# Loading the adjacency matrix in pieces of two tiles

## Chip, core and metric

The kernel runs on one core of a Trainium2 chip. The metric is the device time of one execution in microseconds; the kernel before took 733.56 us, the median of three runs (727.32 to 735.38).

The core has a tensor engine (TensorE, in the profile PE; its weight loads are PEld), a vector engine (VectorE, DVE), a scalar engine (ScalarE, ACT), GpSimd (POOL), and 16 DMA engines that queues on SP, ACT and POOL feed.

## The reference

Two graph layers over 3327 nodes with 512 features. `adj` is a sparse 3327 x 3327 matrix held densely in fp32, more populated towards low node numbers. Cut to what matters:

```python
# layer 0
h = max(layernorm(x), 0)
x = x + (adj @ (relu(adj @ (h @ W1) + b1) @ W2) + b2)
# layer 1
h = max(layernorm(x), 0)
attn_a = sigmoid(concat(adj @ h, h) @ Wa.T + ba)      # attn_b the same, with Wb and bb
hs = h @ W_sa
e = where(adj != 0, exp(-leaky_relu(s_left[:, None] + s_right[None, :])), 0)
x_a = (e / (sum(e, axis=1) + 1e-5)) @ hs
x_b = adj @ (h @ W_gcnb) + b_gcnb
x = x + sigmoid(attn_a * x_a + attn_b * x_b)
```

`adj` is thus used as a dense matrix in two successive products of layer 0, and layer 1 needs the places of its nonzero entries.

## The kernel before

The nodes are padded to 3328, which is 26 blocks of 128, and `adj` comes in transposed as `adjT`. The output columns of a pass are cut into chunks of 512 (`CW`); 3328 is six and a half of them, so one chunk has a width of 256.

**First pass** (lines 549 to 600). For each chunk, from the last columns to the first, TensorE sums `acc_u` over the 26 row blocks `j`: `u[j]`, which is `h @ W1` of block `j`, against the tile of `adjT` at rows `j` and the chunk's columns (line 568). The same tiles serve the lists of nonzeros: VectorE takes for each row and each group of 32 columns the largest absolute value (line 572), into `most[:, group, j]`. In the first chunk the loads of x, the layer norm, the transposes and the products that make `u` are woven in between.

When a chunk ends, `make_g` takes its sum with relu on ScalarE (line 343), transposes it and copies it to `g`; `make_lists` is made for the chunk and advanced, one step behind each tile, through the next chunk: flags from `most`, a running count (line 452), two small matmuls (lines 465 to 476), masks `at` on VectorE (line 502), short matmuls with these masks into `p_list` (line 513), and `past`, `jb`, `row_h` and `row_a` on VectorE (lines 519 to 532), the numbers of the rows that are to be gathered. GpSimd issues gathers of parts of `adjT` by these numbers (line 166), each paced behind a matmul of the pass. The generator's statements stand in the program where the loop calls it, but the tile framework's scheduler orders the instructions of each engine anew from its own estimate of times, with the constraints that `queued` and `issue_after` set.

**Second pass** (lines 818 to 856). For the dense chunks (four of width 512 and one of 256) TensorE sums `acc_g` over the blocks in the order of the chunks of the first pass, `g[j]` against the tile of `adjT` (line 825). The two other chunks are summed from gathered rows (`acc_s`, line 784). Between these matmuls stand `px` (line 663), which makes x of layer 1 from a finished chunk, its layer norm, and `acc_hub` (line 709), the first block's sums of layer 1. x is loaded again on SP's queue (line 648), and the rows of h are stored there (line 637).

**Layer 1** follows, with the gathered rows only: `acc` (line 981), transposes, `p_b` (line 1035), `p_a` (line 1042) and the output. It doesn't use the dense tiles.

Both passes load the tiles through `load_adj` (line 271), one DMA on SP's queue for each call, 256 KB: one tile in a full chunk and two in the half-width one. Its pool `adjp` has eight buffers of 128 x 512 fp32. A load waits until every instruction that used its buffer is done: the matmul, and in the first pass the maximum too. SP's queue is in order, so what stands behind a waiting load waits with it.

Of the kernel before, what the change touches and what calls it, by code (L numbers as in the profile page):

```python
# [9 lines left out]
F32 = mybir.dt.float32  # L10
AF = mybir.ActivationFunctionType
ALU = mybir.AluOpType
# [4 lines left out]
AX = mybir.AxisListType  # L17

P = 128
CW = 512  # L20
GW = 32
# [29 lines left out]
def kernel(  # L51
# [17 lines left out]
    nc = tc.nc  # L69
    NP, D = x.shape  # L70
    HID = W1.shape[1]
    NB = NP // P
# [25 lines left out]
    def bank(pool, name):  # L98
        return pool.tile([P, CW], F32, tag="bank", name=name)
# [116 lines left out]
    def gather_behind(matmul):  # L216

        g = next(columns, None)
        if g is not None:
            pace(g, matmul)  # L220

    def queued(*insts):

        behind = ExitStack()
        for inst in insts:
            if inst is not None:
                behind.enter_context(tc.issue_after(inst.ins))
        return behind
# [30 lines left out]
    with (  # L259
        tc.tile_pool(name="l0", bufs=1) as l0,  # L260
        tc.tile_pool(name="l0w", bufs=2) as l0w,
        tc.tile_pool(name="adjp", bufs=8) as adjp,
    ):

        def load_adj(j, c, name, n=1):

            c0, w = c
            t = adjp.tile([P, CW], F32, tag="adj", name=f"{name}_{c0}_{j}")
            t = t[:, : n * w].rearrange("p (k i) -> p k i", i=w)
            rows = adjT[j * P : (j + n) * P, c0 : c0 + w]  # L270
            nc.sync.dma_start(t, rows.rearrange("(k p) i -> p k i", p=P))
            return t
# [22 lines left out]
        def load_weights():  # L295
            nc.scalar.dma_start(W2_sb, W2)
            nc.scalar.dma_start(b2_row, b2.partition_broadcast(P))
            nc.scalar.dma_start(W_sa_sb, W_sa.rearrange("(k p) f -> p k f", p=P))
            nc.scalar.dma_start(w_own, w_self.partition_broadcast(P))
            nc.scalar.dma_start(bab_row, b_ab.partition_broadcast(P))  # L300
# [4 lines left out]
        x_loaded, scaled, h_turned, u_made = {}, {}, {}, {}  # L305

        def load_x(i):
            xs[i] = l0w.tile([P, D], F32, tag="x", name=f"x_{i}", bufs=5)
            x_loaded[i] = nc.sync.dma_start(xs[i], x[i * P : (i + 1) * P, :])

        def normalize(i):

            hs[i] = l0w.tile([P, D], F32, tag="h", name=f"h_{i}", bufs=GR // NU)
            with tc.high_priority():
                scaled[i], _ = ln_relu(
                    hs[i], xs.pop(i), l0w, f"a{i}", [scaled.get(i - 2)],
                    [h_turned.get(i - 3), u_made.get(i - 4)],
                    [h_turned.get(i - 2), u_made.get(i - 3)],
                )

        def turn_h(i):
            h = hs.pop(i)
            pt = bank(psB, f"pt_{i}")
            for k in range(KD):
                nc.tensor.transpose(pt[:, k * P : (k + 1) * P], h[:, k * P : (k + 1) * P], ident)  # L325
            hs[i] = hTs[i % 2]
            h_turned[i] = nc.scalar.copy(hs[i].rearrange("p k n -> p (k n)"), pt)

        def make_u(i):
            hT = hs.pop(i)  # L330
            pu = bank(psB, f"pu_{i}")
            for k in range(KD):
                nc.tensor.matmul(  # L333
                    pu[:, :HID], hT[:, k, :], W1_sb[:, k, :], start=(k == 0), stop=(k == KD - 1)
                )
            u_made[i] = nc.scalar.copy(u[i], pu[:, :HID])
# [212 lines left out]
        for n, c in enumerate(back):  # L549
            c0, w = c  # L550
            acc = bank(psA, f"acc_u_{c0}")
            per = CW // w
            most = l0w.tile([P, MG, NB], F32, tag="most", name=f"most_{c0}")
            for j in range(NB):
                if n == 0:
                    if j + 4 < NB:
                        load_x(j + 4)
                    if j + 3 < NB:
                        normalize(j + 3)
                    if j + 2 < NB:  # L560
                        turn_h(j + 2)
                    if j + 1 < NB:
                        make_u(j + 1)
                if j % per == 0:
                    with queued(x_loaded[min(j + 4, NB - 1)] if n == 0 else None):
                        tile_a = load_adj(j, c, "a1", per)
                a = tile_a[:, j % per, :]
                added = nc.tensor.matmul(  # L568
                    acc[:, :w], u[j], a[:, :w], start=(j == 0), stop=(j == NB - 1)
                )  # L570
                with queued(scaled[min(j + 3, NB - 1)] if n == 0 else None):
                    nc.vector.tensor_reduce(  # L572
                        most[:, : w // GW, j], a[:, :w].rearrange("p (b i) -> p b i", i=GW),
                        axis=AX.X, op=ALU.max, apply_absolute_value=True,
                    )
                if j >= 2:
                    next(lists, None)
                if j % 4 if w == CW else j % 2:
                    gather_behind(added)
                if n == 0 and j % 2 == 0:  # L580
                    with queued(scaled[min(j + 3, NB - 1)]):
                        next(constants, None)
            for work in (lists, constants):
                for _ in work:
                    pass
            chunk_end = make_g(c, acc)
            with tc.issue_after(chunk_end.ins):
                if n == 1:
                    load_weights()
                if 0 < n <= HUB_LOADS:  # L590
                    load_hub(n - 1)
                for i in OWN:
                    if n and c0 <= i * P < c0 + w:
                        load_own(i)
            lists = make_lists(n, most)
            next(lists)
# [208 lines left out]
        def next_late():  # L805
            while late:
                try:
                    next(late[0])
                    return
                except StopIteration:  # L810
                    late.pop(0)
# [6 lines left out]
        for c, (c0, w) in enumerate(dense_chunks):  # L818
            last = c == len(dense_chunks) - 1
            acc = bank(psA, f"acc_g_{c0}")  # L820
            per = CW // w
            for n, j in enumerate(order):
                if n % per == 0:
                    a = load_adj(j, (c0, w), "a2", per)
                added = nc.tensor.matmul(  # L825
                    acc[:, :w], g[j], a[:, n % per, :], start=(n == 0), stop=(n == NB - 1)
                )
                if c == 0 and n >= 2:
                    next(lists, None)
                if n in SUMS.get(c, ()):  # L830
                    next(summing)
                elif c and n % 4:
                    gather_behind(added)
                if n % 2 or (c in (2, 3) and n % 4 == 2):
                    with queued(last_e[0] if last and n < 8 else None):
                        next_late()
                if last and n >= NB - QUIET:
                    continue
                if c > 1 and n % 3 == 2:
                    next(hubs)  # L840
                elif c > 1 and (n > 8 if last else n % 3 == 1):
                    with queued(last_row[0] if last else None):
                        make_e_hub()
            if c == 0:
                for _ in lists:
                    pass
                nc.vector.tensor_reduce(overflow, size, axis=AX.X, op=ALU.max)
            if last:
                with queued(last_e[0]):
                    nc.scalar.activation(root, eps, AF.Sqrt)  # L850
                while late:
                    next_late()
            sT = l0w.tile([HID, CW], F32, tag="gT", name=f"sT_{c0}", bufs=3)
            nc.scalar.copy(sT[:, :w], acc[:, :w])
            late.append(make_h1((c0, w), sT, last))
# [47 lines left out]
    with tc.tile_pool(name="spw", bufs=2) as spw:  # L903
# [175 lines left out]
        with queued(made[1]):  # L1079
            ty, _ = copy_out(0, acc_hub)  # L1080
# [7 lines left out]
        for i in range(NB - 2, 1, -1):  # L1088
# [8 lines left out]
            b, ty, es = turning  # L1097
# [19 lines left out]
        b, ty, es = turning  # L1117
# [19 lines left out]
        ty, _ = copy_out(1, taken[1]["acc"], True)  # L1137
# [3 lines left out]
    with tc.If(over > 0):  # L1141
        with (
# [19 lines left out]
            for c0, w in listed_chunks:  # L1162
                acc = bank(psA, f"acc_again_{c0}")
                for j in range(NB):
                    a = load_some(j, c0, w, "a5")
# [5 lines left out]
                for b in range(w // P):  # L1171
                    i = c0 // P + b
# [23 lines left out]
        with (  # L1196
# [25 lines left out]
            for c in range(len(chunks)):  # L1222
                c0, w = chunks[c]
# [10 lines left out]
                for j in range(NB):  # L1234
                    a = load_all(j, c, "a3")
# [9 lines left out]
                for j in range(NB):  # L1245
                    a = load_all(j, c, "a4")
# [10 lines left out]
                for b in range(w // P):  # L1257
                    i = c0 // P + b
# [63 lines left out]
```

## Time and profile before

The profiled execution took 834.5 us, of which 832.8 us are its span. It is one execution under the profiler; the median of the timed runs is 733.56 us.

| | before |
|---|---|
| median of three runs | 733.56 us |
| profiled execution, its span | 834.5 us, 832.8 us |
| matmuls busy (PE) | 735.6 us, 88% |
| VectorE busy | 506.0 us, 61% |
| ScalarE busy | 194.5 us, 23% |
| GpSimd busy | 461.1 us, 55% |
| loads of adj tiles | 286, 256 KB each |
| maxima (line 572) | 182, of them 156 over 512 elements |
| matmuls of the first pass (line 568) | 161.0 us |
| matmuls of the second pass (line 825) | 117.1 us |
| bytes read from HBM, and mean rate of all DMA | 162.29 MB, 222 GB/s |

A row of the groups reads: line, engine, operation, output and input with their shapes, how often; then busy time and mean ns of one; then the idle time of the engine just before them and what ended most of it. An fp32 matmul leaves two records. A row of the chain that ended last gives start, length and what was on the path. A row of waits gives who waited for whom, the total, how often, and the longest. Busy time counts whatever an engine does, on the path or beside it, so the profile is best read stage by stage.

### The profile page before, as it was taken

The numbers are of one execution on the slowest core, as the hardware profiler recorded it, in microseconds if no ns is written. First come the engines' busy times: TensorE is split into PE (matmuls) and PEld (weight loads), VectorE is DVE, ScalarE is ACT, GpSimd is POOL, SyncE is SP. The second block draws the span as 40 slices with busy tenths as digits, with TensorE's granted clock in tenths as the row PEclk, the third lists the DMA queues.
The fourth block names the chain that finished last, engine by engine and source line by source line (L and its number), as shares of the span: only waits on it lengthen the run. The fifth ranks groups of instructions, "written<-read, shape, count | busy, mean of one in ns | idle before, by whom it ended". The sixth has DMA issues, their size and how long they took to land.

```text
span 832.8 us, 11907 instructions
## 1 busy us (share of the span) xinstructions
PE 735.6 (88%) x3595; PEld 404.5 (49%) x3595; DVE 506.0 (61%) x1625; ACT 194.5 (23%) x402; POOL 461.1 (55%) x490
## 2 busy tenths in 40 slices
PE   9999888989899771999899749967999999999995
PEld 7774333444543220444355236633656655665554
DVE  7778868898860611798987225523665557553552
ACT  7770000000000110354544002211212222221121
POOL 2201756766657776534456766674657666767500
PEclk9999989999999875999999969996999999999999
DMA  8788988988878844789994755664667877767510
GB/s 271 245 287 259 326 246 242 293 272 246 232 232 284 262 132 134 240 279 312 327 314 135 241 150 145 199 185 115 195 211 244 255 206 233 240 205 234 178 51 29
DMA packets 104889, 185.08 MB, mean 222 GB/s; under 512 B 18401, under 2 KB 35441, under 8 KB 104818
## 3 DMA queue, kind: packets, MB, share of 16 engines
q1 hardware_dynamic: 66544, 113.43, 41.8%
q0 software_dynamic: 23264, 57.64, 24.3%
q10 hardware_dynamic: 15010, 13.18, 4.9%
q8 instruction: 30, 0.49, 0.2%
q14 instruction: 41, 0.34, 0.1%
HBM read 162.29 MB, written 22.26 MB: 222 GB/s over the span
## 4 chain that ended last, share of the span: by engine, by line
PE 72%; DVE 7%; issue 6%; another core or an unknown queue 6%; DMA 5%; ACT 2%; POOL 1%; SPq 1%; DVEq 0%; ACTq 0%; POOLq 0%
PE acc_u L568 17%; PE acc L981 12%; PE p_b L1035 11%; PE p_a L1042 10%; PE acc_g L825 8%; PE pu L333 3%; PE ptt L995 3%; DMA a<-in_adjT_dram 2%; PE acc_hub L709 2%; PE px L663 2%; PE pt L325 1%; DMA xb<-in_x_dram 1%; PE acc_s L784 1%; DMA hr<-h_rows,row_h 1%
## 5 line engine op out<-in xcount | busy, mean ns | idle before, releaser
L166 POOL DMA_INDIRECT ae<-in_adjT_dram,row_a x194 | 202.6, 1044 | 181.8 <-DVE past L519 54.3
L568 PE MATMUL acc_u<-a,rows 128*128 128x512 f32 (+1 forms) x364 | 161.0, 583 | 0.5 <-DMA a<-in_adjT_dram 0.5
L166 POOL DMA_INDIRECT hr<-h_rows,row_h x120 | 122.7, 1022 | 62.5 <-issue 27.4
L825 PE MATMUL acc_g<-a,g 128*128 128x512 f32 (+1 forms) x260 | 117.1, 584 | 7.2 <-DMA a<-in_adjT_dram 6.8
L572 DVE TENSOR_REDUCE most<-a 128x16 f32<-128x512 f32 (+1 forms) x182 | 112.3, 638 | 11.6 <-issue 6.3
L1035 PE MATMUL p_b<-W_g_sb,tyT 128*128 128x257 f32 x416 | 99.3, 391 | 15.8 <-DVE tyT L1010 15.3
L1035 PEld LDWEIGHTS p_b<-W_g_sb,tyT 128*128 128x128 f32 x416 | 77.8, 192 | 46.5 <-DVE tyT L1010 15.6
L166 POOL DMA_INDIRECT rows<-h_rows,row_h x74 | 75.1, 1015 | 44.3 <-PE acc L981 20.9
L568 PEld LDWEIGHTS acc_u<-a,rows 128*128 128x128 f32 x364 | 67.2, 195 | 58.8 <-issue 56.0
L1042 PE MATMUL p_a<-W_sa_sb,tyT 128*128 128x512 f32 (+2 forms) x216 | 94.2, 577 | 0.2
L1010 DVE COPY tyT<-ptt 128x512 f32<-128x512 f32 x51 | 34.8, 685 | 87.0 <-PE p_a L1042 31.7
L825 PEld LDWEIGHTS acc_g<-a,g 128*128 128x128 f32 x260 | 50.0, 200 | 58.5 <-issue 44.9
L981 PE MATMUL acc<-hr,ae 64*64 64x512 f32 x480 | 68.3, 614 | 4.4 <-issue 4.0
L166 POOL DMA_INDIRECT g_row<-g_rows,row_h x48 | 49.0, 1021 | 20.9 <-issue 13.4
L1042 PEld LDWEIGHTS p_a<-W_sa_sb,tyT 128*128 128x128 f32 x216 | 40.7, 189 | 38.8 <-issue 36.9
L884 ACT ACTIVATE f<-f 128x2 f32<-128x2 f32 x26 | 5.3, 203 | 192.4 <-DVE f L883 97.2
L981 PEld LDWEIGHTS acc<-hr,ae 64*64 64x64 f32 x480 | 27.6, 136 | 33.6 <-issue 33.0
L343 ACT ACTIVATE gT<-acc_u,b_col 128x512 f32<-128x512 f32 (+1 forms) x7 | 4.6, 656 | 163.8 <-DMA a<-in_adjT_dram 90.9
L663 PE MATMUL px<-W_sb,sT 128*128 128x512 f32 x52 | 26.7, 650 | 15.4 <-ACT sT L799 12.0
L666 DVE TENSOR_TENSOR xb<-px,xb 128x512 f32<-128x512 f32 x26 | 17.3, 682 | 36.6 <-PE px L663 28.5
L981 PE MATMUL acc<-rows,ae 64*64 64x512 f32 x296 | 37.1, 593 | 2.5 <-issue 2.3
L623 DVE SCALAR_TENSOR_TENSOR junk<-rows,w_rows 128x512 bf16<-128x512 f32 x52 | 35.6, 684 | 3.2 <-ACT rows L244 1.1
(159 smaller groups left out, 945.2 us busy)
## 6 DMA issues: line engine op xcount, KB each, us to landing
a<-in_adjT_dram SPq DMA_DIRECT2D x286, 256.0 KB
h_rows<-rows SPq DMA_DIRECT2D x26, 260.0 KB
x<-in_x_dram SPq DMA_DIRECT2D x26, 256.0 KB
xb<-in_x_dram SPq DMA_DIRECT2D x26, 256.0 KB
x<-xb ACTq DMA_DIRECT2D x26, 256.0 KB
x1b<-x SPq DMA_DIRECT2D x26, 256.0 KB
out_dram<-va SPq DMA_DIRECT2D x25, 256.0 KB
ae<-in_adjT_dram,row_a POOLq DMA_INDIRECT x194
```

What stands on the lines that cost most here:

```text
L166: return nc.gpsimd.indirect_dma_start(out=dst, out_offset=None, in_=table, in_offset=bass.IndirectOffsetOnAxis(ap=rows, axis=0), bounds_ch ...
L333: nc.tensor.matmul(pu[:, :HID], hT[:, k, :], W1_sb[:, k, :], start=(k == 0), stop=(k == KD - 1))
L568: added = nc.tensor.matmul(acc[:, :w], u[j], a[:, :w], start=(j == 0), stop=(j == NB - 1))
L572: nc.vector.tensor_reduce(most[:, : w // GW, j], a[:, :w].rearrange("p (b i) -> p b i", i=GW), axis=AX.X, op=ALU.max, apply_absolute_value ...
L623: return nc.vector.scalar_tensor_tensor(junk, h, 1.0, w_rows[:, s, :], op0=ALU.mult, op1=ALU.mult, accum_out=into)
L663: last_row[2] = nc.tensor.matmul(px, sT[:, b * P : (b + 1) * P], W2_sb, start=True, stop=True)
L825: added = nc.tensor.matmul(acc[:, :w], g[j], a[:, n % per, :], start=(n == 0), stop=(n == NB - 1))
L981: added = nc.tensor.matmul(taken[i]["acc"][h][q * HALF : (q + 1) * HALF, :], both[half_p, q * n + k, :], taken[i][k0][k][half_p, q, :D], s ...
L995: moved = nc.tensor.transpose(pt[:, k * P : (k + 1) * P], ty[h][:, k * P : (k + 1) * P], ident)
L1010: last = nc.vector.tensor_copy(dst, src)
L1035: nc.tensor.matmul(p_b[n][:, :WH], tyT[:, k, 0, :], W_g_sb[:, k, n * WH : (n + 1) * WH], start=(k == 0), stop=(k == KD - 1),)
L1042: last = nc.tensor.matmul(p_a[:, c0:c1], tyT[:, k, 1, :], W_sa_sb[:, k, c0:c1], start=(k == 0), stop=(k == KD - 1),)
```

## The change

Each load of adj takes two tiles in a full chunk and four in the half-width one (512 KB), the last one of a half-width chunk only the two that are left. The pool has four buffers of twice the size, the same bytes as before. From the second chunk of the first pass on, one instruction of VectorE takes the maxima of two tiles; in the first chunk it is one tile for each instruction as before. The matmuls are the same.

```diff
-        tc.tile_pool(name="adjp", bufs=8) as adjp,
+        tc.tile_pool(name="adjp", bufs=4) as adjp,
...
-            t = adjp.tile([P, CW], F32, tag="adj", name=f"{name}_{c0}_{j}")
+            t = adjp.tile([P, 2 * CW], F32, tag="adj", name=f"{name}_{c0}_{j}")
...
-            per = CW // w
+            per = 2 * CW // w
...
                 if j % per == 0:
                     with queued(x_loaded[min(j + 4, NB - 1)] if n == 0 else None):
-                        tile_a = load_adj(j, c, "a1", per)
+                        tile_a = load_adj(j, c, "a1", min(per, NB - j))
...
-                with queued(scaled[min(j + 3, NB - 1)] if n == 0 else None):
-                    nc.vector.tensor_reduce(
-                        most[:, : w // GW, j], a[:, :w].rearrange("p (b i) -> p b i", i=GW),
-                        axis=AX.X, op=ALU.max, apply_absolute_value=True,
-                    )
+                both = 2 if n else 1
+                if j % both == 0:
+                    tiles = tile_a[:, j % per : j % per + both, :]
+                    with queued(scaled[min(j + 3, NB - 1)] if n == 0 else None):
+                        nc.vector.tensor_reduce(
+                            most[:, : w // GW, j : j + both],
+                            tiles.rearrange("p k (b i) -> p b k i", i=GW),
+                            axis=AX.X, op=ALU.max, apply_absolute_value=True,
+                        )
...
-            per = CW // w
+            per = 2 * CW // w
             for n, j in enumerate(order):
                 if n % per == 0:
-                    a = load_adj(j, (c0, w), "a2", per)
+                    a = load_adj(j, (c0, w), "a2", min(per, NB - n))
```

## The prediction

> **What bounds the kernel now.** I read the page first for the totals and then cut the span at the ScalarE evictions of line 343, which end the chunks of the first pass (65.1, 89.6, 124.4, 154.9, 182.5, 212.5 and 231.6 us). The windows view of these stretches, with the busy time of PE, PEld, DVE, ACT and POOL, the granted clock, the DMA share and GB/s, says most:
>
> ```profile
> PE 735.6 (88%) x3595; PEld 404.5 (49%) x3595; DVE 506.0 (61%) x1625; ACT 194.5 (23%) x402; POOL 461.1 (55%) x490
> ```
>
> ```profile
> 65.00:89.50 24.50, 24.50 (x109) 11.09 (x108) 22.15 (x56) 0.69 (x1) 7.09 (x7) 1.00 0.89 280
> 89.50:124.40 34.90, 27.58 (x109) 12.49 (x108) 26.32 (x68) 0.69 (x1) 23.00 (x23) 0.85 0.90 284
> 124.40:154.90 30.50, 26.90 (x109) 11.97 (x108) 25.28 (x65) 0.70 (x2) 19.86 (x21) 0.94 0.86 258
> 154.90:182.50 27.60, 25.72 (x116) 11.81 (x115) 25.01 (x67) 0.67 (x1) 18.70 (x19) 1.00 0.89 277
> 182.50:212.50 30.00, 28.01 (x125) 12.80 (x124) 26.32 (x66) 0.70 (x2) 20.24 (x21) 0.94 0.87 262
> 212.50:231.60 19.10, 16.35 (x152) 12.07 (x151) 15.58 (x52) 0.68 (x2) 12.05 (x13) 1.00 0.71 200
> ```
>
> The second chunk (65.0 to 89.5) has TensorE busy all through: 24.5 us is what its 26 tiles and its share of the lists cost it. The later full chunks take 27.6 to 34.9 us. In them VectorE works 25.0 to 26.3 us, and the DMA engines 0.86 to 0.90 of the time, which is 24.6 to 26.2 us in the three chunks after the one that also brings the weights. So three servers need about 25 us each for a chunk, and what lies above that is their waiting for one another.
>
> The chain that ended last (start, length, what) shows which side gives way where:
>
> ```profile
> 79.02 8.79 PE acc_u L568 x20
> 89.55 4.72 DMA a<-in_adjT_dram
> ...
> 113.91 11.36 PE acc_u L568 x26
> ...
> 135.00 3.58 DMA a<-in_adjT_dram
> ...
> 247.33 4.41 DMA a<-in_adjT_dram
> ...
> 274.24 2.41 DMA a<-in_adjT_dram
> ```
>
> The stretch of 26 records is 13 tiles (two records for each fp32 matmul): 11.36 / 13 = 0.874 us per tile, or 262,144 B / 0.874 us = 300 GB/s that adj alone has to come at. Where the chain leaves TensorE it goes through a load of `a`, whose 256 KB took 2.4 to 4.7 us from issue to landing. The DMA queue's own waits say what those loads wait for (total us, times, longest):
>
> ```profile
> SPq L271 <- PE acc_u L568: 52.9, 58, 3.7
> SPq L271 <- PE acc_g L825: 38.3, 42, 6.4
> SPq L271 <- DVE most L572: 8.3, 6, 2.5
> ```
>
> They wait for buffers, which the matmuls, and sometimes the maxima, give back. The eight buffers are therefore in use, and how early one comes back is the lead that a load has. The maxima by shape:
>
> ```profile
> L572 DVE TENSOR_REDUCE most<-a 128x16 f32<-128x512 f32 x156 | 102.7, 676 | 11.3 <-issue 6.0 <-DMA a<-in_adjT_dram 5.0
> L572 DVE TENSOR_REDUCE most<-a 128x8 f32<-128x256 f32 x26 | 9.6, 408 | 0.3 <-issue 0.3
> ```
>
> **What the Trainium skill says.** "Perfetto Trace Analysis", section "Optimizing Scalar/DVE Operations": an instruction of VectorE on SBUF pays some 60 ns beside its elements, and about twice that in the profiled duration, since part of it overlaps the next. The trace agrees: the chain has two maxima back to back in 1.19 us (0.595 each) and six of the half-width ones in 1.96 us (0.327), so an element costs (0.595 - 0.327) / 256 = 1.05 ns and an instruction 0.059 us. The durations, 676 and 408 ns, give 140 ns. The same page, "DMA Optimizations", names both sides of the load: larger DMAs use the HBM better, smaller pieces let work start sooner. Here the runs stay 2 KB (1 KB in half-width chunks), so I count nothing on the first side. "DMA: Bandwidth & Descriptors", section "Anatomy of one DMA — SWDGE (gpsimd) path", puts most of a 2 us fixed cost in the confirmation of the last byte. It speaks of the other issue path, but the shortest landing here (2.41 us, with 0.87 us for the bytes at 300 GB/s) leaves 1.5 us, which fits.
>
> **The maxima in pairs.** Five chunks of 13 pairs and a half-width one of 13: 78 instructions fewer. At 0.059 us each that is 4.6 us; by the durations, 78 x 0.140 = 10.9 us. I take 4.6 us, since VectorE is nearly always followed at once here, and keep both ends. It lies on the path only where VectorE is the last of the three, and then counts in full (0.8 us a chunk). The pair also has to wait for two tiles, but that moves nothing else: in the order of the built programs the first 36 list matmuls (line 513) need the masks `at` (line 502) that stood behind the maxima of 9 tiles and now stand behind 5 pairs: 9 x 0.595 = 5.36 us against 5 x (1024 x 1.05 ns + 0.059) = 5.67 us, 0.3 us later; the other 12 stood behind 13 maxima (7.74 us) and stand behind 7 pairs (7.94). TensorE has by then passed those tiles. Cost 0 to 0.3 us per chunk, 1 us in all; I take 0.
>
> **The loads in pairs.** 286 issues become 144. SP saves 142 x 0.33 us of issue time (the median on its queue), but SP is no step of the path, so 0. What changes is the lead. Before, a buffer returns when its tile is used and its new tile is needed seven tiles later: 7 x 0.874 = 6.1 us, against 0.33 us to issue plus 2.4 to 4.7 us to land, a slack of 1.1 to 3.4 us. After, a buffer returns when the second of its tiles is used, and is needed six tiles later: 5.2 us; and its landing has 0.87 us more bytes in it: 0.33 + 3.3 to 5.6 us. The slack is -0.7 to +1.6 us. A slack of -0.7 us costs 0.7 us in each round of eight tiles. Behind the first chunk there are 6 chunks in the first pass and 5 in the second, two of them of half width: 10 full chunks x 26 / 8 = 32 rounds. None of them short costs 0, all of them 23 us. The two long landings (4.4 and 4.7) among the four in the chain would be short after the change and the two short ones not, but the chain shows the loaded moments, and the second pass has slower tiles from its second chunk on. I take 14 rounds, under half: 14 x 0.7 = 10 us.
>
> Where a load is late anyway, TensorE now waits for the second tile of a pair before it can start the first, one tile of 0.87 us; the chain has four such places: 3 us (0 to 3.5).
>
> **What moves on SP's queue.** Behind a load that waits for its buffer stand the loads of x and the stores of h rows (lines 648 and 637). In the orders, some of these come one tile earlier and some one tile later against the loads; each is some 0.9 us and they cancel: 0, bounded by 2 us to either side, because two loads of x are on the chain (5.3 us at 376.8, 5.2 at 394.3). The scheduler also puts the last products `junk_w` (line 606) into the first pass, where TensorE waited 0.9 us for one at the start of the second: -0.9 us at best, 0 taken. First chunk: its tile cost is 2.19 us on TensorE (0.44 + 0.89 + 0.86 in the chain), which hides a coarser load.
>
> **Sum.** -4.6 x 0.9 (VectorE is among the last in most, not all, chunks) = -4; +10; +3: +9 us, rounded down to +8. The profiled execution took 834.5 us (span 832.8), 101 us over the median of 733.56. Much of its waiting is absent from timed runs, but the three equal floors are not, so I carry the difference and not the ratio: 733.6 + 8 = **742 us**.
>
> **Rivals.**
> - *VectorE decides.* Its 25.0 to 26.3 us stand above the 24.5 us that TensorE needs in each chunk from the third on; whatever it is relieved of shortens the chunk as long as it remains above TensorE and DMA. That ends not slower: -4.6 to -10.9, middle -8, 726 us. It decides if loads keep landing within 5.2 us less issue, that is if the pair lands in under 4.9 us. For it: TensorE waits at the list matmuls for `at` and `most`. Against: the DMA engines' 24.6 to 26.2 us stand right below, and the saving that is sure is 0.8 us a chunk.
> - *Both are hidden.* Most loads land in the short time (2.4 to 3.6 us, slack 0.4 to 1.6 after), so the lead suffices; VectorE's gain of 4 meets 3 us for the pairs waited for, and 1 us of the order: 733 us. For it: TensorE waited directly for `a` only 0.5 us in the first pass and 6.8 in the second.
> - *Every round is short*: 23 + 3 - 4 = +22, 756 us. It needs landings above 4.9 us throughout, for which only the half of the samples speaks.
> - That the pairs aren't made is excluded: the orders show 13 double-width maxima per chunk and 144 loads.
>
> **Numbers.** Slower by the lead (742): 0.43; all rounds short (756): 0.05; both hidden (733): 0.38; VectorE decides (726): 0.14. Range 726 to 756, both outer cases at its ends. One per cent (7.3 us) is about what a measurement of this kernel tells from no change; the faster case lies just beyond it and half of the slower case's neighbours within it, so: faster 0.12, within 0.42, slower 0.46.
>
> **What would show it.** Right: SP's waits for `acc_u` and `acc_g` grow per load, new waits of TensorE or VectorE for `a` in the first pass of together 5 us or more, chunks longer than before. Wrong: chunks nearer 24.5 us with VectorE at 24 us or less, and a pair that lands under 4.9 us. The maxima should show about 1.2 us for 1024 elements; well above that would take the gain away, well below it would add to it.

## The result

The changed kernel takes 741.38 us (median of 12 runs, 736.99 to 746.98), the kernel before in the same comparison 732.38 us (12 runs): a ratio of 1.0116 with a 95% interval of 1.0083 to 1.0149, so 8.5 us slower by the ratio. A second comparison gave 741.11 against 733.84 us, 1.0106 (1.0062 to 1.0150).

The kernel before takes 732 to 735 us on some chips and 835 us on another, where the granted clock of TensorE is lower (0.95 of full speed against 0.99, means over its runs); the profile shown ahead of the prediction (834.5 us, clock 0.94) looks like the slower kind, and its chain of work has stretches of up to 16.5 us put down to an unknown queue. So the comparisons below are made within runs on one chip, and the profile of the kernel before was taken once more on a faster chip; that execution took 730.81 us, its span 729.1.

The windows view of the first pass behind its first chunk, cut at the ScalarE evictions of line 343 as before (busy time of PE, PEld, DVE, ACT and POOL, clock, DMA share, GB/s), first for the kernel before on a faster chip:

```profile
65.19:89.67 24.48, 24.48 (x108) 11.07 (x107) 22.24 (x56) 0.69 (x1) 7.15 (x7) 1.00 0.90 280
89.67:120.40 30.73, 26.82 (x108) 10.42 (x107) 24.42 (x62) 0.69 (x2) 23.73 (x24) 1.00 0.97 312
120.40:146.82 26.42, 24.87 (x108) 11.05 (x107) 26.42 (x71) 0.68 (x1) 18.70 (x20) 1.00 0.98 304
146.82:172.06 25.24, 25.15 (x116) 11.44 (x115) 25.24 (x67) 0.69 (x2) 19.49 (x19) 1.00 0.98 310
172.06:197.95 25.89, 25.07 (x125) 11.29 (x124) 25.61 (x65) 0.69 (x2) 20.37 (x19) 1.00 0.99 302
197.95:214.99 17.04, 16.09 (x152) 11.92 (x151) 16.49 (x57) 0.68 (x1) 13.08 (x14) 1.00 0.84 239
```

and for the changed kernel (span 739.9):

```profile
65.28:90.17 24.89, 24.71 (x107) 10.60 (x105) 21.18 (x44) 0.69 (x1) 7.15 (x7) 1.00 0.86 270
90.17:124.04 33.87, 29.73 (x108) 12.98 (x109) 26.42 (x56) 0.69 (x1) 23.11 (x23) 0.85 0.93 292
124.04:151.15 27.11, 25.75 (x107) 10.54 (x105) 25.23 (x55) 0.69 (x1) 19.80 (x21) 1.00 0.94 287
151.15:178.95 27.80, 26.13 (x116) 11.41 (x117) 25.72 (x55) 0.69 (x2) 19.26 (x19) 1.00 0.92 281
178.95:206.08 27.13, 25.64 (x125) 11.18 (x124) 24.99 (x53) 0.69 (x1) 19.84 (x20) 1.00 0.94 285
206.08:224.65 18.57, 17.14 (x151) 11.59 (x149) 17.24 (x47) 0.69 (x2) 13.71 (x14) 1.00 0.76 211
```

These six chunks take 149.8 us before and 159.4 after. The second pass, up to its last eviction (line 854, then 858), takes 169.5 us before (384.5 - 215.0) and 170.1 after (394.7 - 224.6; 172.1 in the second profile of the changed kernel). Layer 1 is the same length within 1.3 us. So by these profiles nearly all of the loss lies in the first pass.

In the three full chunks from 120 us on, the kernel before has VectorE busy all the time but 0.3 us, TensorE for 25 of 25 to 26 us, and the DMA engines at 0.98 to 0.99. After the change none of the three is full: VectorE, busy for 25.3 us a chunk in place of 25.8, idles for about 2 us of it, and the DMA share is 0.92 to 0.94. The rate falls from 302 to 310 down to 281 to 287 GB/s. Share and rate fall with any chunk that moves the same bytes in a longer time: the share times the length is 25 to 26 us in all six rows. So they show that time is lost, and not by what.

The chunk from 90 us on, which also brings weights, is 3.1 us longer, and its clock is 0.85 in place of 1.00. Whether its waits led to the lower clock, or the clock to a part of its length, isn't shown. The other five chunks are 6.4 us longer. Over the timed runs the clock of the changed kernel is not lower (0.992 on average against 0.990), so a lower clock doesn't explain its loss.

The chain that ended last, of the changed kernel:

```profile
92.82 9.41 DMA a<-in_adjT_dram
...
124.04 6.63 DMA a<-in_adjT_dram
130.75 4.78 DMA a<-in_adjT_dram
135.55 1.22 DVE most L575
...
145.93 5.59 DMA a<-in_adjT_dram
151.55 1.22 DVE most L575
...
225.62 4.43 DMA a<-in_adjT_dram
```

and two of the loads on the chain of the kernel before, in its new profile:

```profile
191.87 3.49 DMA a<-in_adjT_dram
...
248.76 6.68 DMA a<-in_adjT_dram
```

A landing on the chain now takes 4.4 to 9.4 us, and the maximum of a pair often stands behind it. In the kernel before these landings are 3.5 to 6.7 us. A chain that ended last picks the late loads, so these aren't typical ones. The waits of SP's queue, of the changed kernel:

```profile
SPq L271 <- PE acc_u L568: 73.3, 62, 3.9
SPq L271 <- PE acc_g L829: 72.0, 42, 4.0
SPq L271 <- DVE most L575: 44.9, 42, 4.1
```

For each of 144 loads that is (73.3 + 72.0 + 44.9) / 144 = 1.3 us of waiting for a buffer. The kernel before, on a faster chip too:

```profile
SPq L271 <- PE acc_u L568: 53.6, 101, 1.8
SPq L271 <- PE acc_g L825: 51.8, 71, 3.3
SPq L271 <- DMA a<-in_adjT_dram: 26.2, 26, 2.8
SPq L271 <- DVE most L572: 13.6, 21, 1.6
```

Here it is (53.6 + 51.8 + 13.6) / 286 = 0.4 us. A load is twice as large after the change, so for each tile it is 0.7 against 0.4 us. (The waits put down to another load's landing, 26.2 us here and 12.0 us after the change, are left out of both.) The wait for a buffer is put down to VectorE twice as often as before, 42 times in place of 21. The maxima of the changed kernel, by shape:

```profile
L575 DVE TENSOR_REDUCE most<-a 128x32 f32<-128x1024 f32 x65 | 78.9, 1214 | 17.2 <-DMA a<-in_adjT_dram 16.9
```

### The profile page after: what moved, and what is told of

It reads as the page before. It is cut to its first block, busy times and chain, and to the rows that moved or that the text cites. A ratio compares the mean times of both kernels' runs of the same rounds, so it can differ in the third digit from the quotient of the medians.

```text
span 739.9 us, 11529 instructions
## 1 busy us (share of the span) xinstructions
PE 707.0 (96%) x3595; PEld 392.0 (53%) x3595; DVE 502.2 (68%) x1547; ACT 193.6 (26%) x402; POOL 467.9 (63%) x490
## 4 chain that ended last, share of the span: by engine, by line
PE 73%; DMA 13%; DVE 10%; ACT 2%; issue 1%; POOL 0%; DVEq 0%; SPq 0%; ACTq 0%; POOLq 0%
PE acc_u L568 13%; PE acc L985 13%; PE p_b L1039 13%; PE p_a L1046 12%; DMA a<-in_adjT_dram 8%; PE acc_g L829 7%; PE pu L333 3%; PE ptt L999 3%; DVE most L575 2%; DMA xb<-in_x_dram 2%; PE px L667 2%; DVE junk L627 2%; PE pt L325 2%; PE acc_hub L713 1%; DMA x<-xb 1%
## 5 line engine op out<-in xcount | busy, mean ns | idle before, releaser
L568 PE MATMUL acc_u<-a,rows 128*128 128x512 f32 (+1 forms) x364 | 164.7, 584 | 4.6 <-DMA a<-in_adjT_dram 4.3
L575 DVE TENSOR_REDUCE most<-a 128x32 f32<-128x1024 f32 (+1 forms) x104 | 104.6, 1010 | 17.2 <-DMA a<-in_adjT_dram 16.9
L829 PE MATMUL acc_g<-a,g 128*128 128x512 f32 (+1 forms) x260 | 110.5, 556 | 3.0 <-DMA a<-in_adjT_dram 2.9
L568 PEld LDWEIGHTS acc_u<-a,rows 128*128 128x128 f32 x364 | 64.9, 194 | 62.6 <-issue 43.0
L1039 PE MATMUL p_b<-W_g_sb,tyT 128*128 128x257 f32 x416 | 97.1, 385 | 0.8 <-ACT tyT L1012 0.5
L829 PEld LDWEIGHTS acc_g<-a,g 128*128 128x128 f32 x260 | 47.3, 190 | 52.2 <-issue 40.6
L166 POOL DMA_INDIRECT g_row<-g_rows,row_h x48 | 51.7, 1077 | 20.8 <-issue 12.8
L985 PE MATMUL acc<-hr,ae 64*64 64x512 f32 x480 | 57.1, 593 | 0.0
L343 ACT ACTIVATE gT<-acc_u,b_col 128x512 f32<-128x512 f32 (+1 forms) x7 | 4.6, 657 | 156.7 <-DMA a<-in_adjT_dram 113.2
L985 PEld LDWEIGHTS acc<-hr,ae 64*64 64x64 f32 x480 | 25.9, 134 | 20.1 <-issue 20.0
L999 PEld LDWEIGHTS ptt<-ident,ty 128*128 128x128 f32 x208 | 24.2, 141 | 14.2 <-issue 13.4
```

The lines of the kernel that those rows point to most:

```text
L166: return nc.gpsimd.indirect_dma_start(out=dst, out_offset=None, in_=table, in_offset=bass.IndirectOffsetOnAxis(ap=rows, axis=0), bounds_ch ...
L568: added = nc.tensor.matmul(acc[:, :w], u[j], a[:, :w], start=(j == 0), stop=(j == NB - 1))
L575: nc.vector.tensor_reduce(most[:, : w // GW, j : j + both], tiles.rearrange("p k (b i) -> p b k i", i=GW), axis=AX.X, op=ALU.max, apply_ab ...
L829: added = nc.tensor.matmul(acc[:, :w], g[j], a[:, n % per, :], start=(n == 0), stop=(n == NB - 1))
L985: added = nc.tensor.matmul(taken[i]["acc"][h][q * HALF : (q + 1) * HALF, :], both[half_p, q * n + k, :], taken[i][k0][k][half_p, q, :D], s ...
L999: moved = nc.tensor.transpose(pt[:, k * P : (k + 1) * P], ty[h][:, k * P : (k + 1) * P], ident)
```

## The experiments

The ratios below are to the kernel before on the same chip.

### One part alone: loads in pairs, maxima of one tile

```diff
-                both = 2 if n else 1
+                both = 1
```

> The changed kernel with the maxima of one tile each; only the loads are in pairs. Lead theory: the changed kernel plus the 4 us that the maxima save: 745. Rival, VectorE is hidden: 741. Rival, the maxima of two tiles are what costs: 732.

On the chip with before at 835 us: 839.95 against 835.17 us, 1.0054 (1.0015 to 1.0092).

> Loads in pairs, maxima of one tile. Lead theory as recorded: 745 where before is at 732. If the cost is in the maxima of two tiles and the loads in pairs are hidden: 732 to 736. If each part alone makes the lead one tile shorter and both together do no more than that: some 738 to 741, as the ring and the changed kernel.

On a chip with before at 733.84 us: 740.60 us, 1.0094 (1.0064 to 1.0123). Beside it the changed kernel:

> The changed kernel, for a comparison on the same chip with its single parts: 1.2% over the kernel before where that takes 732 us. Where the kernel before takes 835 us, the lead theory has the same 9 us, 844; if waits without a visible releaser hide the loads there, less.

It took 741.11 us, 1.0106. So nearly all of the loss comes with the loads in pairs, 6.8 us, and the maxima of two tiles neither give back the 4 us that I expected of them (745 forecast, 740.6 measured) nor add anything that these intervals tell. It is the third of the cases above that came. The first pass behind its first chunk takes 155.8 us here, 6.0 more than before, and the second 173.6, 4.1 more. The chunk that brings the weights is as long as before, at a clock of 1.00:

```profile
90.66:121.54 30.88, 25.56 (x108) 10.73 (x107) 25.97 (x67) 0.69 (x1) 22.40 (x22) 1.00 0.98 316
```

### The other part alone: single loads, maxima of two tiles

The pool becomes one ring of eight tiles, so that two neighbouring tiles can be read by one instruction; every load is one tile as before.

```diff
-            t = adjp.tile([P, CW], F32, tag="adj", name=f"{name}_{c0}_{j}")
-            t = t[:, : n * w].rearrange("p (k i) -> p k i", i=w)
+            slot = len(loads) % RING
+            loads.append(slot)
+            t = ring[:, slot, : n * w].rearrange("p (k i) -> p k i", i=w)
...
+                both = 2 if n else 1
+                if n == 0 or j % 2:
+                    tiles = ring[:, loads[-1] + 1 - both : loads[-1] + 1, :]
+                    if w < CW:
+                        tiles = tile_a
```

> The kernel before with its eight single-tile loads, kept in one ring of eight tiles so that the maxima can be taken of two neighbouring tiles from the second chunk on. Only VectorE's part of the change is made. Lead theory (the pairs of loads cost some 13 us, the maxima gain 4): 4 us under the kernel before, 728 against 732. Rival, the maxima or the new order of instructions are what costs: as slow as the changed kernel, 741. Rival, VectorE decides: 726 or less.

On the chip with before at 835 us: 845.54 us, 1.0116 (1.0074 to 1.0158). That is against the theory, so it was measured again where the kernel before takes 733.84 us:

> Single loads in a ring of eight, maxima of two tiles. It came out 1.2% slower on a chip on which the kernel before takes 835 us, against what the lead theory said. If the maxima of two tiles cost time everywhere (a tile of the pair comes back to the loads later, and a p_list matmul waits for more): 738 to 742 where before is at 732. If that was the other chip's doing and VectorE's saving counts: 728 to 731.

737.84 us, 1.0059 (1.0038 to 1.0081), 4.0 us slower. The ring itself could have been the cause:

> Single loads in a ring of eight tiles, maxima of one tile each: what the kernel before computes, with its pool written as a ring. If the 0.6% that the ring with maxima of two tiles cost come from the maxima: as before, ratio 1.000 within 0.002. If they come from the ring: 1.005 or more.

733.67 against 734.62 us, 0.9991 (0.9967 to 1.0016): the ring costs nothing that this interval tells, and the maxima of two tiles, with the order of instructions that the scheduler makes for them, cost 0.6%. The waits of VectorE for tiles point to how; first the ring with maxima of one tile, then of two:

```profile
DVE most L576 <- DMA ring<-in_adjT_dram: 10.6, 14, 2.1
```

```profile
DVE most L581 <- DMA ring<-in_adjT_dram: 17.0, 18, 2.3
```

VectorE waits 6.4 us more for tiles than with single maxima, which is more than what the pairs save. A pair can't start until its second tile is there, what is queued behind it on VectorE waits too, and the first tile's buffer comes back only with the pair. The six chunks of the first pass take 156.3 us in this kernel, 149.4 in the ring with single maxima. A rival isn't excluded: the clock of this kernel is lower than that of the kernel before on the same chip (0.9856 on average against 0.9901). Among the kernel before's own 24 runs there, 0.001 less of the clock goes with some 0.5 us more, so about 2 of the 4 us, an estimate, go along with the clock, and whether the waits lower it isn't shown. Its full chunks also show that a lower DMA share and rate are no mark of large loads:

```profile
150.32:177.47 27.15, 25.10 (x116) 11.03 (x115) 24.83 (x54) 0.69 (x2) 19.23 (x20) 1.00 0.93 286
```

### Landing or lead: a pair of buffers filled by two DMAs

```diff
-            nc.sync.dma_start(t, rows.rearrange("(k p) i -> p k i", p=P))
+            rows = rows.rearrange("(k p) i -> p k i", p=P)
+            step = CW // w
+            for k in range(0, n, step):
+                nc.sync.dma_start(t[:, k : min(k + step, n), :], rows[:, k : min(k + step, n), :])
```

> The changed kernel with each pair of tiles filled by two DMAs of 256 KB in place of one of 512 KB; the pair of buffers still comes back as one. The landing of the first tile is as early as before, only the lead is one tile shorter. Lead theory: slack 5.2 - 0.33 - (2.4 to 4.7) = 0.2 to 2.5 us, hardly ever short, and no wait for the second tile of a pair: 731 to 735. Rival, the later return of the buffers alone costs the time: 740. Rival, the maxima cost it: 741.

Before at 835 us: 842.64 us, 1.0085 (1.0055 to 1.0115).

> The changed kernel with two DMAs of 256 KB for each pair of buffers; on a chip with before at 835 us it took 1.0085. If the later return of the buffers is what costs: nearly as slow as the changed kernel, ratio 1.008 to 1.012. If the later landing of a 512 KB piece is what costs: 0.998 to 1.003.

Before at 734.62 us: 738.69 us, 1.0061 (1.0033 to 1.0088). It is in neither of the two ranges expected. Against the 1.0106 of the changed kernel, measured on another chip, this brings back nearly half, though the two intervals overlap. The pieces are smaller and the first tile lands earlier, and which of the two helps isn't told. The rest, which stays with pairs that come back as one and maxima of two, is what the ring with maxima of two costs too (1.0059). By the profiles, the first pass gains 2.7 us (156.7 in place of 159.4) and the second is at 170.3 us.

### A shorter lead: six single buffers

```diff
-        tc.tile_pool(name="adjp", bufs=8) as adjp,
+        tc.tile_pool(name="adjp", bufs=6) as adjp,
```

> The kernel before with six buffers in place of eight: a load's lead is 5 tiles, 4.4 us, against 0.33 + 2.4 to 4.7 us, slack -0.7 to +1.7, which is what pairs have. Lead theory: some 10 us slower than before, 742. Rival, the lead is long enough and the cost lies elsewhere in the pairs: 732 to 734.

Before at 835 us: 846.01 us, 1.0103 (1.0043 to 1.0163).

> The kernel before with six buffers in place of eight, all else alike; 1.010 on a chip with before at 835 us. Lead theory: the lead of five tiles is as short as that of the pairs: 1.009 to 1.013. Rival, eight buffers are more than is needed and the pairs cost by their size: 1.000 to 1.003.

Before at 733.84 us: 743.73 us, 1.0145 (1.0100 to 1.0190), 9.9 us by the medians. No load and no maximum is changed here, only the number of buffers, and with it the lead, by two tiles. The scheduler's order isn't quite the same, though: at 69 us VectorE has six masks in a row where the kernel before has ten, and loads of x stand at other places on SP's queue in the second pass. The windows view has its full chunks from the fourth on, and then the second pass:

```profile
122.07:150.18 28.11, 26.01 (x108) 10.81 (x107) 25.92 (x67) 0.69 (x2) 19.89 (x20) 1.00 0.93 282
150.18:177.01 26.83, 25.80 (x116) 11.01 (x115) 25.42 (x66) 0.68 (x1) 18.64 (x20) 1.00 0.93 286
177.01:203.76 26.75, 25.45 (x125) 10.89 (x124) 25.47 (x66) 0.69 (x2) 19.12 (x20) 1.00 0.94 289
222.31:398.10 175.79, 164.32 (x638) 76.39 (x639) 128.30 (x424) 59.15 (x108) 124.61 (x114) 0.99 0.94 304
```

The chunks are as long as those of the changed kernel (26.8 to 28.1 us). The six chunks of the first pass together take 157.4 us, 7.6 more than before. The second pass takes 175.8 us, 6.3 more than before. The loads in pairs alone lose in both passes too, 6.0 and 4.1 us, while the changed kernel loses only 0.6 to 2.6 us in the second. So these six buffers are no exact stand-in for the changed kernel.

### The kernel before, profiled again

> The kernel before once more, for a profile on the same chip as the runs beside it. Lead theory: on a chip on which it takes some 732 us, loads of a land in 2.4 to 4.9 us and TensorE and VectorE wait for them clearly less than in the changed kernel, where the waits of VectorE for a are 16.9 us and those of PE and PEld for it some 25 us. Rival, the lead isn't what costs: the same waits as in the changed kernel.

730.81 us. Its landings on the chain are 3.5 to 6.7 us, longer than expected. VectorE waits less for `a`, all of it in the first pass:

```profile
DVE most L572 <- DMA a<-in_adjT_dram: 11.0, 18, 1.5
```

in place of 16.9 us. The weight loads wait 5.5 us less and the matmuls 1.9 us, most of it in the second pass: 27.1 us for the two together, where the changed kernel has 34.5 (and not the 25 expected). So the waits are less than in the changed kernel, but not clearly so.

### More tiles for the maxima of two

```diff
-        RING = 8
+        RING = 10
...
-    GR = 24
+    GR = 20
```

with two in place of three buffers for gT and sT.

> Single loads in a ring of ten tiles, maxima of two tiles from the second chunk on; the room comes from one buffer less for gT and sT and from 20 in place of 24 rows of g gathered ahead. With eight tiles the maxima of two cost 0.6%. If that is because both tiles are held until the pair's maximum is done, two more tiles make it up and VectorE's saving of some 4 us counts: ratio 0.992 to 0.998. If the maxima of two tiles cost by themselves (VectorE waits for the second tile with list work behind it): 1.003 to 1.006 still.

747.57 against 733.84 us, 1.0192 (1.0149 to 1.0236): the highest ratio of all. The chunks of the first pass behind its first get 153.5 us, 2.9 less than with eight tiles, but the second pass takes 182.4 us in place of 169.8. TensorE's waits in it:

```profile
PE acc_s L794 <- DMA g_row<-g_rows,row_h: 11.3, 5, 7.8
```

That wait isn't in the list of the ring of eight, so the 20 rows gathered ahead may be what the room cost. The two edits for it weren't tried apart, and the clock of this kernel is the lowest of all on the faster chips (0.977 on average against 0.990). The first pass fits the view that held tiles are part of what the maxima of two cost, but it is one profile, and whether more tiles would turn VectorE's saving into time stays open.

## Why the prediction was right

The direction and the size came out: 742 forecast, 741.4 measured, and the range holds it. (The terms sum to +9 us, put at +8; 8.5 were measured.) It is the loads in pairs that make the kernel slower, as forecast. That the size fits so well is luck: the sum's terms fared differently, and two errors in them cancelled.

- *The lead.* 10 us forecast, 14 rounds of 0.7. Six single buffers, whose lead I had put as short as that of the pairs, cost 9.9 us, so a shorter lead does cost time in this kernel, though the order of instructions is not quite the same there. That it is the lead which costs in the pairs is likely and not isolated: the runs with loads of 512 KB have later landings too, and the one with two DMAs has the maxima of two. The count of rounds isn't shown either. It was spread over both passes; the loads in pairs alone lose in both, by one profile, and the changed kernel nearly all in the first. The lead was priced at 0.874 us per tile, while the full chunks of the kernel before run at 1.0 us per tile (25.9 / 26). The landings that I took (2.4 to 4.7 us) were short beside those on the new chains (3.5 to 6.7 before, 4.4 to 9.4 after); over the 145 loads for which a trace has both ends, in the ring of eight with maxima of two, the median is 4.1 us for 256 KB.
- *Waiting for the second tile.* 3 us forecast; splitting the DMA gave back 0.45%, some 3.3 us (1.0106 to 1.0061), but the intervals overlap, and the split makes the landing shorter as well, which belongs to the term above.
- *Together*, the loads in pairs were to cost 13 us and cost 6.8 (4.7 to 9.0): the forecast is nearly twice that.
- *The maxima.* This step failed: "The pair also has to wait for two tiles, but that moves nothing else". The duration was right (1.2 us forecast, 1.214 measured; 1.13 in the chain where one follows another instruction at once), and so was the saving in VectorE's work (506.5 us busy before, 502.2 after). But alone they cost 4.3 us (2.8 to 5.9) in place of saving 4. VectorE waits 6.4 us longer for tiles with them, and the first tile is held until the second is there. I had compared when the list masks come, with both tiles taken as landed. Beside loads in pairs, which make VectorE wait for both tiles anyway, they cost 0.1%, which isn't told from nothing. So two errors, some 6 us too much for the loads and 4 to 5 us too little for the maxima, cancelled.
- *SP's order and the first chunk*, 0 forecast. The first chunk ends at 65.2 to 65.3 us in both. The order on SP's queue wasn't varied by itself; with two DMAs the second pass is within 1 us of the kernel before.
- *The difference carried over.* The profile I had read, 834.5 us, is like those of the chip on which the kernel before takes 835 us; the floors read from it (24.5 us for TensorE, 25 for VectorE, 25 for the DMA engines) are what the full chunks on a faster chip come close to (25.2 to 26.4 us). The changed kernel wasn't run on the slower chip, so that the difference is the same there isn't shown.

Of the signs named in advance, SP's waits for `acc_u` and `acc_g` grew per load (0.4 to 1.0 us), the waits of VectorE for `a` grew by 5.9 us, and the chunks became longer. The waits of TensorE for `a` hardly grew in the first pass.

Of the rivals, *VectorE decides* had its premise: VectorE is busy 26.42 of 26.42 and 25.24 of 25.24 us in two chunks of the kernel before. Its point of decision was a pair that lands in under 4.9 us, and eight of the ten on the chain take longer. *Both are hidden* fell with each part alone: each costs time by itself. *Every round is short* (756) was too far.

## What to carry over

Where several servers are full at once, as in this kernel, count the lead of a load in tiles, from the last user that gives its buffer back to the first that needs it: the same bytes in fewer, larger pieces are a shorter lead, and two fewer of eight buffers cost 9.9 us here. An instruction over two tiles saves its fixed cost but waits for the later one and holds the earlier; price both before the saving is booked, even on the engine that is busiest.

## What was not expected

Landings of 256 KB under this load have a median of 4.1 us (ring of eight with maxima of two) and reach 6.7 us on the chain of the kernel before, with 0.87 us for the bytes at 300 GB/s. The same program takes 14% longer on one chip than on others (835 against 734 us). There the two parts come in another order, the maxima of two alone at 1.0116 and the loads in pairs alone at 1.0054, though the intervals overlap; why is open.
